# Layernorm's inverse deviation by a power on POOL, and gelu written out with Square and Tanh

## The chip, the cores and the metric

The kernel runs on one core of one Trainium2 chip. The metric is the device time of one execution in microseconds (us). Five engines work side by side, each through a list of instructions in a fixed order: TensorE (PE, with its weight loads shown apart as PEld), VectorE (DVE), ScalarE (ACT), GpSimd (POOL) and SyncE (SP, which here issues DMAs). They wait for each other through semaphores.

## The reference

Two transformer layers are run over x of shape (2, 1024, 256), with a context of shape (2, 77, 256). Every sublayer is preceded by a layernorm without weights:

```
def _layernorm(x, axis=-1, eps=1e-05):
    m = jnp.mean(x, axis=axis, keepdims=True)
    v = jnp.var(x, axis=axis, keepdims=True)
    return (x - m) / jnp.sqrt(v + eps)

x = x + L0_xattn(_layernorm(x), ctx)      # cross attention, 16 heads of 16, 77 keys, mask
x = x + L0_ffn(_layernorm(x))             # self attention with 4 heads of 16 chosen by a router
h = jnp.einsum('eth,efh->etf', _layernorm(x), ctx)
x = x + jnp.einsum('etf,efh->eth', jax.nn.gelu(h, approximate=True), ctx)
x = x + moe(_layernorm(x))                # top-1 of 8 experts, 256 -> 1024 -> 256, relu
```

The third sublayer is a feed-forward network whose weights are the context itself: 77 hidden units, with the approximate (tanh) gelu between two matmuls.

## The kernel before, in words

Everything is float32 apart from one mask matmul. The rows are held in SBUF as `xs`, 16 tiles of 128 rows by 256 features, 8 tiles for each of the two batches (`b`). The program runs these stages:

- start: weights are turned on TensorE, and layernorm `a` of batch 0 is written out in two halves of 4 tiles (L399 and L417);
- for each batch: `cross_attention(b)` (with layernorm `a` of batch 1 at its head), then layernorm `b`, then `route_heads(b)`, which averages the normalised rows, makes the router's softmax, picks four heads on VectorE (`nm`, `lg`, `top`, `idx`, `fi`, ..., `seli`) and has SP fetch their weights;
- for each batch: `self_attention(b)`, `context_ffn(b)` (layernorm `c` and the gelu) and `expert_logits(b)` (layernorm `d`, which also writes the normalised and the plain rows to the DRAM tensor `ztok`);
- the ranking of tokens by expert, and the expert blocks, which gather rows from `ztok`.

One layernorm (`layernorm`, `ln_stats`, `ln_rows`, `ln_turn`) works so: for each of 8 tiles VectorE makes statistics (`bn_stats`, `bn_aggr`, into `mv`); ScalarE takes the square root of the 8 variances at once (`sd`, L261); VectorE takes the reciprocal (`rs`, L262) and normalises tile by tile (`y`, L266); TensorE turns each pair of tiles (`lps`, L276), and ScalarE and VectorE in turn copy the result to `yT`. In layernorm `d`, SP writes each `y` to `ztok`, and ScalarE's queue issues the DMA of the plain rows (L297).

The gelu stage handles a batch in two chunks of 512 rows. Each makes `gps` (77 x 512, two matmuls in float32, L782), applies the gelu on ScalarE (`g`, L787), makes four products `gpo` (L790) and adds each to `xs` on VectorE (L794). `gps` and `gpo` share a PSUM pool of two buffers (`accp`), as do most small products.

ScalarE needs the table of a function in place before it can evaluate it. The compiler puts a load (ACT_TABLE_LOAD in the profile) ahead of an instruction whose function is not in the loaded set, and the profile gives it that instruction's line. In the program before there are loads ahead of Sqrt (L261), of Exp (L503, L559, L836), of the gelu (L787) and of the first copy (L370).

POOL has few instructions in the stages of the change: `add_bias` (L303), one addition over 8 tiles (128 x 2048) that must wait until the batch's rows have been read by the layernorm ahead of it, and copies of inverse sums in the self attention.

The order of instructions on each engine is made when the program is built: a planner orders them by estimated times, except in the two stretches under `manual_schedule` (the start and the self attention), where TensorE, VectorE and ScalarE keep the written order. A change of one instruction can thus move others. Once built, the order is fixed.

Of the kernel before, what the change touches and what calls it, by code (L numbers as in the profile page):

```python
# [9 lines left out]
F32 = mybir.dt.float32  # L10
# [3 lines left out]
AF = mybir.ActivationFunctionType  # L14
ALU = mybir.AluOpType
# [5 lines left out]
P = 128  # L21
EPS = 1e-5
NEG = -1e10


def bf16_parts(v):

    parts = []
    for _ in range(3):
        m, e = math.frexp(v)  # L30
        part = math.ldexp(math.trunc(m * 256), e - 8)
        parts.append(part)
        v -= part
    assert v == 0
    return parts
# [3 lines left out]
def kernel(  # L39
# [30 lines left out]
    nc = tc.nc  # L70
# [4 lines left out]
    NT = S // P  # L75
# [20 lines left out]
    const = ctx.enter_context(tc.tile_pool(name="const", bufs=1))  # L96
    keep = ctx.enter_context(tc.tile_pool(name="keep", bufs=1))
    small = ctx.enter_context(tc.tile_pool(name="small", bufs=2))
# [71 lines left out]

    ident = const.tile([P, P], F32, name="ident")
    make_identity(nc, ident)
    eps_t = const.tile([P, 1], F32, name="eps_t")
    nc.vector.memset(eps_t, EPS)


    ztok = dram.tile([B * S, 2 * D], F32, name="ztok")

    hmask = const.tile([P, HG], F32, name="hmask")
    nc.gpsimd.memset(hmask, float(HD) ** -0.5)
# [31 lines left out]
    neg3 = const.tile([P, 1], F32, name="neg3")  # L214
    parts = bf16_parts(NEG)
    nc.gpsimd.memset(neg3, 0.0)
# [36 lines left out]
    ynp = work.enter_context(tc.tile_pool(name="ynp", bufs=4))  # L253


    def ln_stats(b, tag, mv, sd, rs, t0, t1):
        for t in range(t0, t1):
            st = small.tile([P, 6], F32, name=f"st_{tag}{b}_{t}", tag="st", bufs=4)
            nc.vector.bn_stats(st, xs[:, b * NT + t, :])
            nc.vector.bn_aggr(mv[:, t, :], st)  # L260
        nc.scalar.activation(sd[:, t0:t1], mv[:, t0:t1, 1], AF.Sqrt, bias=eps_t)  # L261
        nc.vector.reciprocal(rs[:, t0:t1], sd[:, t0:t1])  # L262

    def ln_rows(b, tag, mv, rs, t):
        y = ynp.tile([P, D], F32, name=f"y_{tag}{b}_{t}", tag="y")
        nc.vector.tensor_scalar(  # L266
            y, xs[:, b * NT + t, :], mv[:, t, 0:1], rs[:, t : t + 1],
            ALU.subtract, ALU.mult,
        )
        return y  # L270

    def ln_turn(b, tag, yT, t0, ys, copy):
        ps = trp.tile([P, C, 2, P], F32, name=f"lps_{tag}{b}_{t0}", tag="tr")
        for i, y in enumerate(ys):
            for c in range(C):
                nc.tensor.transpose(ps[:, c, i, :], y[:, c * P : (c + 1) * P], ident)  # L276
        copy(yT[:, :, t0 * P : (t0 + 2) * P], ps.rearrange("p c t k -> p c (t k)"))

    def ln_tiles(b, tag):
        mv = small.tile([P, NT, 2], F32, name=f"mv_{tag}{b}", tag="mv")  # L280
        sd = small.tile([P, NT], F32, name=f"sd_{tag}{b}", tag="sd")
        rs = small.tile([P, NT], F32, name=f"rs_{tag}{b}", tag="rs")
        yT = ytp.tile([P, C, S], F32, name=f"yT_{tag}{b}", tag="yT")
        return mv, sd, rs, yT

    def layernorm(b, tag, y_out=None):

        mv, sd, rs, yT = ln_tiles(b, tag)
        ln_stats(b, tag, mv, sd, rs, 0, NT)
        for t0 in range(0, NT, 2):  # L290
            ys = []
            for t in (t0, t0 + 1):
                ys.append(ln_rows(b, tag, mv, rs, t))
                if y_out is not None:
                    r0 = (b * NT + t) * P
                    nc.sync.dma_start(y_out[r0 : r0 + P, :D], ys[-1])
                    nc.scalar.dma_start(y_out[r0 : r0 + P, D:], xs[:, b * NT + t, :])  # L297
            ln_turn(b, tag, yT, t0, ys, evac)
        return yT
# [42 lines left out]
    def queries(b, yT, n):  # L342

        for m in range(C):
            ps = accp.tile([P, 512], F32, name=f"qps_{b}_{m}_{n}", tag="acc")
            for c in range(C):
                nc.tensor.matmul(
                    ps,
                    lhsT=wT["q"][:, c, m * P : (m + 1) * P],
                    rhs=yT[:, c, n : n + 512],  # L350
                    start=(c == 0),
                    stop=(c == C - 1),
                )
            nc.scalar.activation(
                qT[:, m, n : n + 512], ps, AF.Identity, bias=bq_c[:, m : m + 1]
            )
# [4 lines left out]
    def turn_weight(nm, copy):  # L361

        t = wT[nm] = const.tile([P, C, D], F32, name=f"w{nm}T")
        ps = trp.tile([P, C, C, P], F32, name=f"wps_{nm}", tag="tr")
        for ci in range(C):
            for co in range(C):
                nc.tensor.transpose(
                    ps[:, ci, co, :], raw[nm][:, co, ci * P : (ci + 1) * P], ident
                )
        copy(t.rearrange("p c d -> p (c d)"), ps.rearrange("p a b k -> p (a b k)"))  # L370
# [8 lines left out]
    def context_k(m, eng):  # L379
        ps = accp.tile([P, B, KC], F32, name=f"kps_{m}", tag="acc")  # L380
        for c in range(C):
            nc.tensor.matmul(
                ps.rearrange("p b k -> p (b k)"),
                lhsT=wT["k"][:, c, m * P : (m + 1) * P],
                rhs=ctxT[:, c].rearrange("p b k -> p (b k)"),
                start=(c == 0),
                stop=(c == C - 1),
            )
        kT = small.tile([P, B, KC], F32, name=f"kT_{m}", tag="kT")
        nc.vector.scalar_tensor_tensor(kT, ps, bk_c[:, m : m + 1], keep01, ALU.add, ALU.mult)  # L390
        for j in range(HG):
            eng.tensor_scalar(kblk[:, :, m, j, :], kT, hmask[:, j : j + 1], None, ALU.mult)

    mv, sd, rs, yT_a = ln_tiles(0, "a")
    with tc.manual_schedule(
        engines={mybir.EngineType.PE, mybir.EngineType.DVE, mybir.EngineType.Activation}
    ):
        turn_weight("q", nc.scalar.copy)
        ln_stats(0, "a", mv, sd, rs, 0, 4)  # L399
        ys = [ln_rows(0, "a", mv, rs, t) for t in range(4)]  # L400
        for b in range(B):
            ps = trp.tile([P, C, KC], F32, name=f"cps_{b}", tag="tr")
            for c in range(C):
                nc.tensor.transpose(ps[:, c, :], ctxs[:, b, c * P : (c + 1) * P], ident[:KC, :KC])
            nc.scalar.copy(ctxT[:, :, b, :], ps)
        turn_weight("k", nc.scalar.copy)
        ln_turn(0, "a", yT_a, 0, ys[:2], nc.scalar.copy)
        ln_turn(0, "a", yT_a, 2, ys[2:], nc.scalar.copy)
        nc.vector.tensor_scalar(keep01, mask_i, 0.0, None, ALU.not_equal)
        context_k(0, nc.vector)  # L410
        context_k(1, nc.gpsimd)
        for j in range(HG):
            nc.vector.tensor_scalar(
                mneg[:, :, j, :], mask_i, 0.0, neg3, ALU.is_equal, ALU.mult
            )
        queries(0, yT_a, 0)
        ln_stats(0, "a", mv, sd, rs, 4, 8)  # L417
        ys = [ln_rows(0, "a", mv, rs, t) for t in range(4, 8)]
        ln_turn(0, "a", yT_a, 4, ys[:2], nc.scalar.copy)
        ln_turn(0, "a", yT_a, 6, ys[2:], nc.vector.tensor_copy)  # L420
        queries(0, yT_a, 512)
# [3 lines left out]
    for b in range(B):  # L425
        ps = accp.tile([KC, D], F32, name=f"vcps_{b}", tag="acc")
        for c in range(C):
            nc.tensor.matmul(
                ps, lhsT=ctxT[:, c, b, :], rhs=wT["v"][:, c, :], start=(c == 0), stop=(c == C - 1)
# [347 lines left out]
    def context_ffn(b):  # L777
        yT = layernorm(b, "c")
        for n in range(0, S, 512):
            ps = accp.tile([KC, 512], F32, name=f"gps_{b}_{n}", tag="acc")  # L780
            for c in range(C):
                nc.tensor.matmul(  # L782
                    ps, lhsT=ctxT[:, c, b, :], rhs=yT[:, c, n : n + 512],
                    start=(c == 0), stop=(c == C - 1),
                )
            g = ap_.tile([KC, 512], F32, name=f"g_{b}_{n}", tag="g")
            nc.scalar.activation(g, ps, AF.Gelu_apprx_tanh)  # L787
            for k in range(4):
                po = accp.tile([P, D], F32, name=f"gpo_{b}_{n}_{k}", tag="acc")
                nc.tensor.matmul(  # L790
                    po, lhsT=g[:, k * P : (k + 1) * P], rhs=ctxs[:, b, :], start=True, stop=True
                )
                xt = xs[:, b * NT + n // P + k, :]
                nc.vector.tensor_tensor(xt, po, xt, ALU.add)  # L794

    ps = trp.tile([P, E * FC], F32, name="b1ps", tag="tr")
    nc.tensor.transpose(ps, b1r, ident[: E * FC, : E * FC])
# [44 lines left out]
    for b in range(B):  # L842
        cross_attention(b)
        yT = layernorm(b, "b")
# [13 lines left out]
    ps = accp.tile([P, T + 1, E], F32, name="rank_ps", tag="acc")  # L858
# [219 lines left out]
```

## Time and profile before

| | |
|---|---|
| median of 3 runs | 691.75 us (690.45 to 695.22) |
| the profiled execution, its own time | 688.27 us |
| its span | 686.5 us |
| mean granted TensorE clock | 0.932 |
| PE busy | 602.5 us (88%), 3645 matmuls |
| PEld busy | 434.2 us (63%) |
| DVE busy | 384.6 us (56%), 874 instructions |
| ACT busy | 216.8 us (32%), 416 instructions |
| POOL busy | 80.6 us (12%), 119 instructions |

The profile is of one execution. A busy TensorE is not one at its peak: its clock can be granted in full (1.00) or in part, and a matmul that waits for a buffer inside a group is merged with its neighbours in the timeline. Groups of instructions are given as line, engine, operation, output <- input, count, then busy time in us, the mean of one in ns, and the engine's idle time just before them with what ended most of it. In the timeline the first two columns are the start and the length in us. Idle time of an engine that is not the limit costs nothing.

By stage, from the trace: the start runs to 30 us, cross attention and routing of both batches to 185, the self attention of batch 0 to 307, gelu and layernorm `d` of batch 0 to 340, the self attention of batch 1 to 471, gelu and layernorm `d` of batch 1 to 503, ranking to 518, the experts to the end.

### The profile page before, as it was taken

The page shows a single profiled execution, that of the slowest core. Times are in us where ns is not written, and L with a number is a line of the kernel's source. Part 1 is how long each engine was busy: PE and PEld are TensorE (multiplying, and loading weights), DVE is VectorE, ACT ScalarE, POOL GpSimd, SP SyncE. Part 2 cuts the span into 40 slices and gives each one's busy share as a digit, 9 for nine tenths or more (in the row PEclk, how much of TensorE's full clock was granted, in tenths as well). Part 3 has the DMA queues.
Part 4 walks back from the last instruction along what each step waited for, and adds up shares of the span by engine and source line. Part 5 has one row for each costly group of instructions (what it writes and reads, how often), then busy time and mean ns, then how long its engine had stood idle before and what let it go on. Part 6 is the DMA issues. An engine that isn't in the chain of part 4 may idle for free. (4 is left out here: it accounts for less than half of the span.)

```text
span 686.5 us, 9833 instructions
## 1 busy us (share of the span) xinstructions
PE 602.5 (88%) x3645; PEld 434.2 (63%) x3645; DVE 384.6 (56%) x874; ACT 216.8 (32%) x416; POOL 80.6 (12%) x119
## 2 busy tenths in 40 slices
PE   5799769995989999987999999998744999999985
PEld 3478645883455555553655555564544998899984
DVE  4599796986546666646455566665560322332421
ACT  3343224332036645523105555542200211111110
POOL 4300050002000000000000000000012122322311
PEclk9999969998999999998799999999655999999998
DMA  8000002000100000001100000000339599999980
GB/s 239 1 1 1 1 0 48 8 1 0 34 21 1 1 1 2 0 1 61 63 0 1 1 1 1 1 0 1 123 111 341 181 330 351 348 373 349 333 308 13
DMA packets 50822, 62.71 MB, mean 91 GB/s; under 512 B 12664, under 2 KB 43859, under 8 KB 50773
## 3 DMA queue, kind: packets, MB, share of 16 engines
q1 hardware_dynamic: 45200, 51.93, 22.8%
q0 software_dynamic: 2560, 7.34, 2.9%
q10 hardware_dynamic: 3013, 2.78, 1.2%
q8 instruction: 30, 0.49, 0.3%
q14 instruction: 19, 0.16, 0.1%
HBM read 55.75 MB, written 6.82 MB: 91 GB/s over the span
## 5 line engine op out<-in xcount | busy, mean ns | idle before, releaser
L680 DVE TENSOR_REDUCE bnm<-bsc 128x1 f32<-128x1024 f32 x64 | 75.4, 1219 | 49.5 <-PE bsc L666 49.5
L682 ACT ACTIVATE be<-bsc,bnm 128x1024 f32<-128x1024 f32 x64 | 70.9, 1112 | 50.3 <-DVE bnm L680 49.2
L692 PEld LDWEIGHTS bpt<-ident,be 128*128 128x128 f32 x512 | 54.9, 140 | 39.0 <-issue 18.6
L998 PE MATMUL ph<-ybT,w1s 128*128 128x128 f32 x640 | 76.6, 279 | 0.0
L998 PEld LDWEIGHTS ph<-ybT,w1s 128*128 128x128 f32 x640 | 74.9, 195 | 2.6 <-DVE ybT L993 2.4
L666 PE MATMUL bsc<-kT,qT 64*128 64x512 f32 x256 | 72.3, 640 | 3.5 <-ACT be L682 3.5
L1015 PE MATMUL epo<-w2s,ehT 128*128 128x256 f32 x320 | 75.2, 379 | 0.0
L1006 DVE TENSOR_SCALAR ehT<-ph,b1s 128x128 f32<-128x128 f32 x80 | 22.5, 344 | 93.7 <-ACT ehT L1004 93.7
L692 PE MATMUL bpt<-ident,be 128*128 128x128 f32 x512 | 70.7, 280 | 3.0 <-DVE beT L693 2.0
L1004 ACT ACTIVATE ehT<-ph,b1s 128x128 f32<-128x128 f32 x80 | 22.9, 369 | 149.5 <-issue 107.8
L693 ACT COPY beT<-bpt 128x512 f32<-128x512 f32 x64 | 37.5, 586 | 89.8 <-PE bpt L692 89.8
L702 PE MATMUL bov<-beT,v 128*64 128x256 f32 x512 | 62.3, 385 | 0.0
L1015 PEld LDWEIGHTS epo<-w2s,ehT 128*128 128x128 f32 x320 | 57.9, 190 | 6.3
L693 DVE COPY beT<-bpt 128x512 f32<-128x512 f32 x64 | 43.5, 684 | 17.2 <-PE bpt L692 17.2
L702 PEld LDWEIGHTS bov<-beT,v 128*64 128x64 f32 x512 | 34.3, 136 | 19.2 <-issue 5.7
L666 PEld LDWEIGHTS bsc<-kT,qT 64*128 64x128 f32 x256 | 26.4, 192 | 29.8 <-issue 19.5
L714 POOL COPY brb<-brc 128x256 f32<-128x256 f32 x16 | 6.4, 402 | 288.9 <-DVE brc L712 202.3
L521 PE MATMUL av<-vblk,eT 128*128 128x51 f32 x320 | 38.9, 269 | 0.1
L521 PEld LDWEIGHTS av<-vblk,eT 128*128 128x128 f32 x320 | 38.1, 192 | 0.9 <-PE po_a L338 0.9
L503 ACT ACTIVATE e<-e 128x616 f32<-128x616 f32 x32 | 23.0, 718 | 37.8 <-DVE e L499 37.8
L1024 POOL DMA_INDIRECT out_dram<-ob,etok x20 | 20.3, 1013 | 85.1 <-DMA out_dram<-ob,etok 64.4
L497 DVE TENSOR_REDUCE mx<-sc 128x8 f32<-128x616 f32 x32 | 25.2, 787 | 4.9 <-PE sc L488 4.6
(227 smaller groups left out, 790.9 us busy)
## 6 DMA issues: line engine op xcount, KB each, us to landing
w1s<-in_L_ffn_w_dram SPq DMA_DIRECT2D x20, 1024.0 KB, 10.4
w2s<-in_L_ffn_w_dram SPq DMA_DIRECT2D x20, 1024.0 KB, 9.8
b2s<-in_L_ffn_b_dram SPq DMA_DIRECT2D x20, 128.0 KB, 9.8
xs<-in_x_dram SPq DMA_DIRECT2D x4, 512.0 KB, 5.8
ztok<-xs ACTq DMA_DIRECT2D x16, 128.0 KB, 1.8
ztok<-y_d SPq DMA_DIRECT2D x16, 128.0 KB, 1.9
ws_q<-in_L_ffn_Wq_dram SPq DMA_DIRECT2D x8, 64.0 KB, 2.0
ws_k<-in_L_ffn_Wk_dram SPq DMA_DIRECT2D x8, 64.0 KB, 2.0
```

The source lines that it names most:

```text
L497: nc.vector.tensor_reduce(mx, scv, AX.X, ALU.max)
L503: nc.scalar.activation(em, em, AF.Exp)
L521: nc.tensor.matmul(av[:, h0 : h0 + HW, :].rearrange("p h d -> p (h d)"), lhsT=eT[:, c, :], rhs=vblk[:, b, c].rearrange("p h d -> p (h d)") ...
L666: nc.tensor.matmul(sc[h][:, n : n + 512], lhsT=qk["q"][m][r, t * P : (t + 1) * P], rhs=qk["k"][m][r, n : n + 512], start=True, stop=True,)
L680: nc.vector.tensor_reduce(nm, sc[h], AX.X, ALU.max, negate=True)
L682: nc.scalar.activation(es[i][:, h], sc[h], AF.Exp, bias=nm, accum_out=sms[g][:, q, s : s + 1])
L692: nc.tensor.transpose(pt[:, k - k0, :], es[i][:, h, k * P : (k + 1) * P], ident)
L693: copy(eTs[gm][:, h, k0 : k0 + 4, q * P : (q + 1) * P], pt)
L702: nc.tensor.matmul(ovs[gm][h * FD : (h + 1) * FD, :], lhsT=v[:, k, 2 * m + h, :], rhs=eTs[gm][:, h, k, :], start=(k == 0), stop=(k == NT - 1),
L998: nc.tensor.matmul(ph[:, f, :], lhsT=ws[n][0][:, c, f * P : (f + 1) * P], rhs=ybT[:, c, :], start=(c == 0), stop=(c == C - 1),)
L1004: nc.scalar.activation(hT[:, f, :], ph[:, f, :], AF.Relu, bias=b1s[:, f : f + 1])
L1015: nc.tensor.matmul(po, lhsT=hT[:, f, :], rhs=w2s[:, f, :], start=(f == 0), stop=(f == FC - 1))
```

## The change

Two edits. In `ln_stats`, VectorE adds the epsilon to the variances and POOL raises the sums to the power -0.5, with a constant tile `minus_half`; the square root on ScalarE and the reciprocal on VectorE go. In `context_ffn`, the gelu function of ScalarE is replaced by its formula, h/2 * (1 + tanh(sqrt(2/pi) * (h + 0.044715 h^3))): Square on ScalarE, a two-input step on VectorE, Tanh on ScalarE, another two-input step on VectorE; the half is applied in the addition to `xs`.

```
+    minus_half = const.tile([P, NT], F32, name="minus_half")
+    nc.gpsimd.memset(minus_half, -0.5)
...
-    def ln_stats(b, tag, mv, sd, rs, t0, t1):
+    def ln_stats(b, tag, mv, rs, t0, t1):
         for t in range(t0, t1):
             st = small.tile([P, 6], F32, name=f"st_{tag}{b}_{t}", tag="st", bufs=4)
             nc.vector.bn_stats(st, xs[:, b * NT + t, :])
             nc.vector.bn_aggr(mv[:, t, :], st)
-        nc.scalar.activation(sd[:, t0:t1], mv[:, t0:t1, 1], AF.Sqrt, bias=eps_t)
-        nc.vector.reciprocal(rs[:, t0:t1], sd[:, t0:t1])
+        nc.vector.tensor_scalar(rs[:, t0:t1], mv[:, t0:t1, 1], EPS, None, ALU.add)
+        nc.gpsimd.tensor_tensor(rs[:, t0:t1], rs[:, t0:t1], minus_half[:, t0:t1], ALU.pow)
...
             g = ap_.tile([KC, 512], F32, name=f"g_{b}_{n}", tag="g")
-            nc.scalar.activation(g, ps, AF.Gelu_apprx_tanh)
+            nc.scalar.activation(g, ps, AF.Square)
+            nc.vector.scalar_tensor_tensor(g, g, 1 / GELU_C, ps, ALU.add, ALU.mult)
+            nc.scalar.activation(g, g, AF.Tanh, scale=math.sqrt(2 / math.pi) * GELU_C)
+            nc.vector.scalar_tensor_tensor(g, g, 1.0, ps, ALU.add, ALU.mult)
...
-                nc.vector.tensor_tensor(xt, po, xt, ALU.add)
+                nc.vector.scalar_tensor_tensor(xt, po, 0.5, xt, ALU.mult, ALU.add)
```

`GELU_C` is 0.044715. The tiles `eps_t` and `sd` go. In the built program, ScalarE's list has one table load (L370), POOL's list has nine powers and one memset more, and the power of batch 1's layernorm `a` stands on POOL's list between the two bias additions of that stage. SP's list is the same.

More of the change, by code (lines that the diff above doesn't have):

```diff
@@ L23 @@
 NEG = -1e10
+GELU_C = 0.044715
 def bf16_parts(v):
@@ L172 @@
     make_identity(nc, ident)
-    eps_t = const.tile([P, 1], F32, name="eps_t")
-    nc.vector.memset(eps_t, EPS)
     ztok = dram.tile([B * S, 2 * D], F32, name="ztok")
+    minus_half = const.tile([P, NT], F32, name="minus_half")
+    nc.gpsimd.memset(minus_half, -0.5)
     hmask = const.tile([P, HG], F32, name="hmask")
@@ L280, in ln_tiles @@
         mv = small.tile([P, NT, 2], F32, name=f"mv_{tag}{b}", tag="mv")
-        sd = small.tile([P, NT], F32, name=f"sd_{tag}{b}", tag="sd")
         rs = small.tile([P, NT], F32, name=f"rs_{tag}{b}", tag="rs")
         yT = ytp.tile([P, C, S], F32, name=f"yT_{tag}{b}", tag="yT")
-        return mv, sd, rs, yT
+        return mv, rs, yT
     def layernorm(b, tag, y_out=None):
-        mv, sd, rs, yT = ln_tiles(b, tag)
-        ln_stats(b, tag, mv, sd, rs, 0, NT)
+        mv, rs, yT = ln_tiles(b, tag)
+        ln_stats(b, tag, mv, rs, 0, NT)
         for t0 in range(0, NT, 2):
@@ L392, in context_k @@
             eng.tensor_scalar(kblk[:, :, m, j, :], kT, hmask[:, j : j + 1], None, ALU.mult)
-    mv, sd, rs, yT_a = ln_tiles(0, "a")
+    mv, rs, yT_a = ln_tiles(0, "a")
     with tc.manual_schedule(
@@ L398 @@
         turn_weight("q", nc.scalar.copy)
-        ln_stats(0, "a", mv, sd, rs, 0, 4)
+        ln_stats(0, "a", mv, rs, 0, 4)
         ys = [ln_rows(0, "a", mv, rs, t) for t in range(4)]
@@ L416 @@
         queries(0, yT_a, 0)
-        ln_stats(0, "a", mv, sd, rs, 4, 8)
+        ln_stats(0, "a", mv, rs, 4, 8)
         ys = [ln_rows(0, "a", mv, rs, t) for t in range(4, 8)]
```

## The prediction

> **What bounds the kernel now.** I read the page first. TensorE is busy for 602.5 of the 686.5 us of the span, so no other engine's total decides; what decides is where TensorE stands still, or runs slowly, for the layernorms and the gelu. The page's chain that ended last covers only the last few microseconds, so it does not help here. Next I read ScalarE's groups by line, for what the change takes away:
>
> ```profile
> L261 ACT ACT_TABLE_LOAD x7 | 9.0, 1283 | 6.7 <-DMA ztok<-xs 6.6
> L559 ACT ACT_TABLE_LOAD x2 | 2.6, 1283 | 0.0
> L787 ACT ACT_TABLE_LOAD x2 | 2.6, 1283 | 0.0
> L836 ACT ACT_TABLE_LOAD x2 | 2.6, 1283 | 0.0
> ```
>
> With one load each at L503 and L370 there are 15 loads, 1283 ns each. In the built order of the changed program only L370's is left: 14 go, 14 x 1.283 = 18.0 us of ScalarE. Are they on the path? The timeline of the first gelu stage (start, length, engine, line; idle before it and what ended it, in brackets):
>
> ```profile
> 302.39 1.28 ACT L261 ACT_TABLE_LOAD   x1
> 307.12 0.30 ACT L261 ACTIVATE sd_c<-mv_c,eps_t 128x8 f32<-128x8 f32 x1 [3.45 <-DVE mv_c L260]
> 307.45 0.20 DVE L262 RECIPROCAL rs_c<-sd_c 128x8 f32<-128x8 f32 x1 [0.37 <-ACT sd_c L261]
> 311.31 1.28 ACT L787 ACT_TABLE_LOAD   x1
> 314.13 0.59 ACT L787 ACTIVATE g<-gps 77x512 f32<-77x512 f32 x1 [1.54 <-PE gps L782]
> 314.77 2.35 PE L790 MATMUL gpo<-ctxs,g 77*128 77x256 f32 x8 [0.68 <-ACT g L787]
> 317.20 1.94 PE L782 MATMUL gps<-yT_c,ctxT 128*77 128x512 f32 x4
> 319.18 0.59 ACT L787 ACTIVATE g<-gps 77x512 f32<-77x512 f32 x1 [4.46 <-DMA ztok<-xs]
> ```
>
> Both loads end before what ScalarE waits for: 3.45 us of idleness follow one, 1.54 us the other. They are hidden. The gelu itself is not: TensorE waits 0.68 us for each of its four runs, and nothing else is in its queue.
>
> Only the layernorm after the gelu has its load on the path, because ScalarE comes to it late, behind four DMA issues:
>
> ```profile
> 323.08 1.28 ACT L261 ACT_TABLE_LOAD   x1 [3.30 <-DMA ztok<-xs]
> 323.67 0.30 DVE L260 BATCH_NORM_AGGREGATE mv_d<-st_d 128x2 f32<-128x6 f32 x2
> 324.38 0.30 ACT L261 ACTIVATE sd_d<-mv_d,eps_t 128x8 f32<-128x8 f32 x1
> 324.95 0.41 DVE L266 TENSOR_SCALAR y_d<-xs,mv_d,rs_d 128x256 f32<-128x256 f32 x1
> ```
>
> **Part 1: the loads.** Statistics end at 323.97 and the square root could start at once, but starts at 324.38: 0.41 us, twice, so 0.8 us of the 18.0 are on the path (counted in part 2's layernorm d). The others are covered: the first L261 load (7.40) by the arrival of raw_k, for which TensorE waits until 9.53; L503's by VectorE's first softmax rows, 3.65 us later; those of layernorm b (78.60 and 156.00) by 2.50 and 2.31 us of idleness behind them; L559's and L836's by 3.5 to 5.1 us of idleness. Without that cover each would cost 1.28 us.
>
> The Trainium skill, "ScalarE: Activation LUTs", section "What ACT_TABLE_LOAD costs", puts a switch at about 1283 ns plus a drain of about 1380 ns; in this trace the root at 8.69 follows the load of 7.40 without a gap, so only the first part shows. By that page 14 switches would be an estimated 37 us of ScalarE, by the row 18.0; the page does not ask what hides them.
>
> **Part 2: the inverse deviation.** Before: root on ScalarE (0.30), reciprocal on VectorE (0.20), about 0.6 us from the last statistics to the first normalised row. After: add on VectorE (0.17, as the small TENSOR_SCALAR rows), power on POOL, and two hand-offs of about 0.05. No row shows a power. Below, a two-input POOL row: 128x2048 takes 4.51 us and 128x64 (L982) 0.40 us, which is 2.07 ns an element above 0.27, so 0.29 us for 8 elements if a power cost as much as an add. Above, the longest two-input row itself, 4.5 us. L982 is the nearest row; with twenty times its price an element the power takes 0.27 + 0.33 = 0.6 us, and I take that. Then 0.17 + 0.10 + 0.6 = 0.88 us.
>
> Place by place: layernorm a of batch 0, first half: covered by raw_k, 0. Second half: 17.85 to 18.55 was 0.70 us, now 0.9: +0.2. b of batch 0: the reciprocal stood behind six bn_stats of batch 1 (84.14, though the root was done at 82.68); in the built order two of those still come ahead, so up to 1 us is gained there, but statistics that moved behind it eat most of it before the routing sums: 0. b of batch 1: 159.55 to 160.16, +0.3. c: +0.3 twice. d: the load's 0.41 goes, 0.98 becomes 0.9: -0.1 for both.
>
> Layernorm a of batch 1 is different, for VectorE's order changes. Today:
>
> ```profile
> 97.64 4.51 POOL L303 TENSOR_TENSOR xs<-xs,bo_b 128x2048 f32<-128x2048 f32 x1 [5.05 <-DVE top L565]
> 97.97 4.22 DVE L569 CAST fi<-idx 128x4 f32<-128x4 uint32 x1
> 102.93 0.68 DVE L109 COPY yT_a<-lps_a 128x512 f32<-128x512 f32 x1
> ```
>
> A cast of 4 elements took 4.22 us and ended with POOL's bias addition; in batch 1 the same cast, with POOL idle, took 0.17. So VectorE's cast stands until POOL is done. In the built order all statistics of batch 1's a come later, the add and the power follow the routing maximum (94.3 instead of 91.5), and the rows are normalised between the routing steps: the first row starts near 95.2 instead of 92.66, the last ends near 100.4 instead of 97.57. The bias addition waits for that last row, runs until 104.9, and holds the routing's last cast (seli), which now stands ahead of the copy of yT_a. That copy ends near 105.7 instead of 103.6: +2.1 us for TensorE's queries. If that cast is not held, 0. On POOL's queue the power stands behind the other bias addition, which ends at 92.6, before the power's input is there. SP's list is unchanged.
>
> **Part 3: the gelu.** One ACTIVATE becomes Square, a two-input VectorE step, Tanh, and another such step, each waiting for the last; the halving rides on the existing addition (0.42 either way). ACTIVATE 0.59. VectorE: 256 elements from PSUM and SBUF take 0.42 (L794), 616 take 0.80 (L499), 1.04 ns an element above 0.16, so 0.69 for 512; the three-operand row L390 lies 0.06 above that line; I take 0.72. Hand-offs 0.03 (307.42 to 307.45). Added: 0.59 + 2 x 0.72 + 3 x 0.03 = 2.12 us, four times, 8.5 us. Both engines are free then. The four ztok issues on ScalarE's queue stay behind the second ACTIVATE, and move with it. TensorE's order in this stage does not change, so nothing fills the gap.
>
> **Part 4: TensorE's clock.** Stretches of 2 us; the third number from the end is the granted clock, the first after the stretch's length TensorE's busy time:
>
> ```profile
> 306.00:308.00 2.00, 0.00 (x0) 0.00 (x0) 1.56 (x7) 0.30 (x1) 0.00 (x0) 1.00 0.00 0
> 308.00:310.00 2.00, 1.80 (x10) 1.20 (x11) 2.00 (x7) 0.59 (x1) 0.00 (x0) 0.93 0.00 0
> 310.00:312.00 2.00, 2.00 (x6) 0.83 (x5) 0.96 (x3) 1.28 (x2) 0.00 (x0) 0.50 0.00 0
> 312.00:314.00 2.00, 2.00 (x7) 1.05 (x5) 0.69 (x1) 0.59 (x1) 0.00 (x0) 0.72 0.00 0
> ```
>
> A pause of 2.21 us (305.95 to 308.16) is followed by half clock from 309.7 to 313.1. Today's pauses of 0.68 us bring none between 313 and 323. They become 0.68 + 2.12 = 2.8 us. I expect one such stretch of 3.4 us more in each batch; at half clock up to half of it is lost, and TensorE also waits within it, so 1.5 us each: 3.0. Bounds: 0 and two stretches in each batch, 6.8.
>
> The Trainium skill, "TensorE: Matmul & The Clock Gate", section "HAM oscillation — how this bites in real kernels", forbids only TensorE pauses over about 3.4 us; by it the 2.8 us pauses cost nothing and the sum would be 3.0 lower. The row above, half clock after 2.21 us, speaks against it.
>
> **Sum.** 0.2 + 0.3 + 0.6 - 0.1 = 1.0 for the layernorms, 2.1 for the cast, 8.5 for the gelu, 3.0 for the clock: +14.6 us. The profiled execution took 688.27 us (span 686.5, 1.8 around it), so 702.9 for its like. It lies 3.5 below the median of the three runs, 691.75; I predict the median: 706.
>
> **Rivals.**
> *Light (699).* The power costs 0.29 (seven places on the path, -2.1), the cast is not held (-2.1), the clock holds (-3.0): +7.4. For it: from 314 to 320 TensorE is busy for 4.47 of 6 us, and the clock holds at 1.00. Against: the 4.22 us row and the row of half clock.
> *Slow power (740).* 4.5 us: 3.9 x 7 more, and the two covered places add some 3.4 and 3.2: +34 over the sum. For it: no row gives a power's price. Against: every POOL row of up to 154 elements is under 0.8 us, DMAs apart. Each 1 us more of power is 7 us.
> *Not slower (689): the loads were on the path after all.* If all 14 end waits, 18.0 - 0.8 = 17.2 come off: 706.4 - 17.2 = 689.2. It decides from twelve of fourteen loads. Against: the idle times after them, above.
> That the change keeps its loads is excluded by the built order: a single one is left.
>
> **How the numbers follow.** Forecast 0.60, light 0.17, slow power 0.20, loads 0.03. The range 698 to 722 holds the forecast with its bounds, the light case, and a power up to about 2.3 us; beyond lie some 0.13 above and 0.05 below. One per cent (6.9 us) is about what a measurement of this kernel tells from no change. Only the loads' case, or a lucky light one, is faster by over that: 0.03; within it lie the light case's lower half and the rest: 0.10; slower: 0.87.
>
> **What would show it.** Right: ScalarE has one table load; Square, VectorE, Tanh, VectorE stand in a row of about 2.7 us with TensorE waiting 2.8 us ahead of the gpo matmuls, four times; the power's row near 0.6 us; the cast of seli near 4 us beside POOL's bias addition; half clock between the two gelu runs. Wrong: a power over 2 us; TensorE's wait ahead of the gelu's second matmul under 2 us; layernorm stages shorter than now.

## The result, and the profile after

The changed kernel takes 718.57 us (median of 5 runs, 716.4 to 731.58) against 691.75: a ratio of 1.040 [1.037, 1.0431]. The forecast was 706 with a range of 698 to 722: the direction and the range held, the size did not. Run again beside the kernel before it gave 1.0406 [1.0352, 1.046]. That repeat's profile is read here (span 718.8, own time 720.6), because in the first profiled execution the expert stage alone was about 12 us longer, which no other run shows.

The groups by line (busy us, mean ns of one; then the engine's idle time just before, and what ended it). Of the kernel before:

```profile
L790 PE MATMUL gpo<-ctxs,g 77*128 77x256 f32 x32 | 9.0, 405 | 3.1 <-ACT g L787 2.7
L276 PE MATMUL lps_d<-ident,y_d 128*128 128x128 f32 x32 | 7.7, 424 | 6.7 <-DVE y_d L266 6.7
L276 PE MATMUL lps_c<-ident,y_c 128*128 128x128 f32 x32 | 7.0, 356 | 4.5 <-DVE y_c L266 4.4
L276 PE MATMUL lps_b<-ident,y_b 128*128 128x128 f32 x32 | 6.2, 344 | 6.8 <-DVE y_b L266 6.7
```

Of the changed kernel:

```profile
L370 ACT ACT_TABLE_LOAD x1 | 1.3, 1283 | 2.5 <-issue 2.5
L263 POOL TENSOR_TENSOR rs_c<-rs_c,minus_half 128x8 f32<-128x8 f32 x2 | 3.3, 1642 | 15.4 <-DVE rs_c L262 15.4
L794 PE MATMUL gpo<-ctxs,g 77*128 77x256 f32 x32 | 12.1, 531 | 11.3 <-DVE g L791 11.1
L277 PE MATMUL lps_d<-ident,y_d 128*128 128x128 f32 x32 | 8.2, 425 | 8.6 <-DVE y_d L267 8.6
L277 PE MATMUL lps_b<-ident,y_b 128*128 128x128 f32 x32 | 7.2, 375 | 8.2 <-DVE y_b L267 8.1
L277 PE MATMUL lps_c<-ident,y_c 128*128 128x128 f32 x32 | 6.9, 384 | 7.2 <-DVE y_c L267 7.2
```

One table load is left of 15, as the built order said. A power of 128x8 takes 1.64 us. TensorE waits 11.1 us for the gelu, 2.7 before.

The timeline of the first gelu stage, after:

```profile
314.73 0.17 DVE L262 TENSOR_SCALAR rs_c<-mv_c 128x8 f32<-128x8 f32 x1
314.98 1.65 POOL L263 TENSOR_TENSOR rs_c<-rs_c,minus_half 128x8 f32<-128x8 f32 x1 [7.70 <-DVE rs_c L262]
316.66 2.04 DVE L267 TENSOR_SCALAR y_c<-xs,mv_c,rs_c 128x256 f32<-128x256 f32 x6 [1.77 <-POOL rs_c L263]
...
322.51 0.59 ACT L788 ACTIVATE g<-gps 77x512 f32<-77x512 f32 x1 [1.85 <-PE gps L782]
323.13 0.68 DVE L789 SCALAR_TENSOR_TENSOR g<-g,gps 77x512 f32<-77x512 f32 x1 [0.79 <-ACT g L788]
323.85 0.63 ACT L790 ACTIVATE g<-g 77x512 f32<-77x512 f32 x1 [0.75 <-DVE g L789]
324.51 0.68 DVE L791 SCALAR_TENSOR_TENSOR g<-g,gps 77x512 f32<-77x512 f32 x1 [0.70 <-ACT g L790]
325.25 2.64 PE L794 MATMUL gpo<-ctxs,g 77*128 77x256 f32 x8 [2.78 <-DVE g L791]
327.77 3.30 PE L782 MATMUL gps<-yT_c,ctxT 128*77 128x512 f32 x4
```

Two things are to be seen. VectorE stands for 1.77 us between its own addition and its first row, for POOL's power; root and reciprocal took 0.6 us in all. And the four steps of the gelu stand in a row from 322.51 to 325.19 with TensorE waiting beside them, 2.78 us.

Layernorm d of batch 0, after; the same stretch took 0.98 us from the statistics to the first row before, and takes 1.96 now (339.37 to 341.33):

```profile
339.40 0.17 DVE L262 TENSOR_SCALAR rs_d<-mv_d 128x8 f32<-128x8 f32 x1
339.65 1.64 POOL L263 TENSOR_TENSOR rs_d<-rs_d,minus_half 128x8 f32<-128x8 f32 x1 [23.03 <-DVE rs_d L262]
341.33 1.38 DVE L267 TENSOR_SCALAR y_d<-xs,mv_d,rs_d 128x256 f32<-128x256 f32 x4 [1.75 <-POOL rs_d L263]
341.89 1.94 PE L277 MATMUL lps_d<-ident,y_d 128*128 128x128 f32 x8 [4.31 <-DVE y_d L267]
```

The cast beside POOL's bias addition, in batch 1's layernorm a, after:

```profile
102.47 4.51 POOL L303 TENSOR_TENSOR xs<-xs,bo_b 128x2048 f32<-128x2048 f32 x1 [4.15 <-DVE at L580]
102.71 4.29 DVE L584 CAST seli<-sel 128x4 int32<-128x4 f32 x1
106.91 0.68 DVE L110 COPY yT_a<-lps_a 128x512 f32<-128x512 f32 x1
```

TensorE's clock in windows of the gelu stage and layernorm d, after (length, TensorE's busy time, ..., the granted clock third from the end):

```profile
326.00:328.00 2.00, 1.91 (x7) 0.85 (x6) 1.67 (x5) 0.00 (x0) 0.00 (x0) 0.79 0.27 89
328.00:330.00 2.00, 2.00 (x3) 0.58 (x3) 1.69 (x8) 0.00 (x0) 0.00 (x0) 0.50 0.51 173
332.00:334.00 2.00, 0.14 (x1) 0.14 (x2) 1.11 (x2) 0.63 (x1) 0.00 (x0) 1.00 0.00 0
346.00:352.00 6.00, 6.00 (x18) 3.69 (x16) 1.47 (x3) 0.21 (x1) 0.00 (x0) 0.50 0.20 67
358.00:360.00 2.00, 1.95 (x12) 1.36 (x11) 1.63 (x6) 0.00 (x0) 0.00 (x0) 1.00 0.00 0
```

A stretch of half clock (327 to 330.5) now lies between the two gelu runs, where there was none. A second, in layernorm d, lasts from 334 to about 358; before it lasted from 323.5 to 333.5.

How far the changed kernel lags behind the one before, at the start of some steps (from the two timelines):

| step | lag, us |
|---|---|
| first scores of batch 0 (L479 before) | 1.7 |
| layernorm b of batch 1, first transpose | 5.4 |
| layernorm c of batch 0 | 9.0 |
| layernorm d of batch 0 | 16.4 |
| first queries of batch 1's self attention | 20.7 |
| layernorm c of batch 1 | 22.2 |
| layernorm d of batch 1 | 29.8 |
| ranking | 31.3 |
| end of the span | 32.3 |

The matmuls are the same 3645, so the 32.3 us split by the page's first lines: TensorE's busy time grew from 602.5 to 616.5 (+14.0: the same matmuls, with the granted clock at 0.908 instead of 0.932) and its idle time by the other 18.3. (The profiled execution of before lies 3.5 us under its median, so by medians the difference is 27 to 28 us.) The idle time is found again in the waits ahead of three groups: the gelu's gpo 8.4 (2.7 to 11.1), the transposes of layernorms b, c and d 6.0 (6.8, 4.5, 6.7 to 8.2, 7.2, 8.6) and those of layernorm a 3.2 (2.5 to 5.7): 17.6 together.

### The profile page after: what moved, and what is told of

Same layout as the page of the kernel before. It is cut to its first block, busy times and chain, and to the rows that moved or that the text cites. A ratio compares the mean times of both kernels' runs of the same rounds, so it can differ in the third digit from the quotient of the medians.

```text
span 729.8 us, 9831 instructions
## 1 busy us (share of the span) xinstructions
PE 620.1 (85%) x3645; PEld 442.3 (61%) x3645; DVE 390.3 (53%) x881; ACT 198.9 (27%) x397; POOL 94.6 (13%) x129
## 3 DMA queue, kind: packets, MB, share of 16 engines
q10 hardware_dynamic: 3013, 2.78, 1.1%
## 5 line engine op out<-in xcount | busy, mean ns | idle before, releaser
L1002 PEld LDWEIGHTS ph<-ybT,w1s 128*128 128x128 f32 x640 | 76.8, 199 | 2.1 <-DVE ybT L997 1.2
L666 PE MATMUL bsc<-kT,qT 64*128 64x512 f32 x256 | 74.0, 639 | 3.5 <-ACT be L682 3.5
L693 DVE COPY beT<-bpt 128x512 f32<-128x512 f32 x64 | 43.7, 686 | 18.0 <-PE bpt L692 17.8
```

What stands on the lines that cost most here:

```text
L666: nc.tensor.matmul(sc[h][:, n : n + 512], lhsT=qk["q"][m][r, t * P : (t + 1) * P], rhs=qk["k"][m][r, n : n + 512], start=True, stop=True,)
L693: copy(eTs[gm][:, h, k0 : k0 + 4, q * P : (q + 1) * P], pt)
L1002: nc.tensor.matmul(ph[:, f, :], lhsT=ws[n][0][:, c, f * P : (f + 1) * P], rhs=ybT[:, c, :], start=(c == 0), stop=(c == C - 1),)
```

## The experiments

They ran on three chips, in groups of four; each ratio is to runs of the kernel before on the same chip, whose median was 692.69 us for the first group, 686.71 for the second and 690.22 for the third. Groups are compared by ratio.

### First group: the parts, one at a time

The changed kernel again, unedited:

> The changed kernel again, for a profile without the longer expert stage of the first one. Theory (a sum of five terms: gelu chain 8.5 us, half clock, power 1.65 us at seven places, moved VectorE steps, and almost nothing back for the loads): about 27 us over the kernel before, with the growth spread over all stages up to the ranking and none behind it (end of the ranking's first matmul about 28 to 31 us later than before, the experts as long as before). Rival (part of the loss lies in the expert stage, as the first profile shows 12 us there): the experts are longer here too.

719.71 us, ratio 1.0406 [1.0352, 1.046].

The gelu alone: the kernel before with only this edit; roots and loads stay.

```
-            nc.scalar.activation(g, ps, AF.Gelu_apprx_tanh)
+            nc.scalar.activation(g, ps, AF.Square)
+            nc.vector.scalar_tensor_tensor(g, g, 1 / GELU_C, ps, ALU.add, ALU.mult)
+            nc.scalar.activation(g, g, AF.Tanh, scale=math.sqrt(2 / math.pi) * GELU_C)
+            nc.vector.scalar_tensor_tensor(g, g, 1.0, ps, ALU.add, ALU.mult)
```

> The kernel before with only the gelu written out; root, reciprocal and all 15 table loads stay (one now stands between Square and Tanh), and TensorE's list is word for word that of before. Theory: 4 x 2.1 = 8.4 us of chain, 2 x 0.55 because the load of 1.28 is longer than the VectorE step of 0.72 beside it, and about 1.7 us of half clock in each batch: +13 us, between 10 and 15. Rival (clock not touched by pauses of 2.8 us): +9.5 us with granted clock 1.00 between the two gelu runs. Rival (second chunk's chain hides behind the first's products): under +5 us.

702.88 us, ratio 1.0188 [1.0133, 1.0244]: 13 us by the ratio (10 by the medians). The timeline of its first gelu run:

```profile
313.55 0.59 ACT L788 ACTIVATE g<-gps 77x512 f32<-77x512 f32 x1 [2.86 <-PE gps L783]
314.15 1.28 ACT L790 ACT_TABLE_LOAD   x1
315.45 0.63 ACT L790 ACTIVATE g<-g 77x512 f32<-77x512 f32 x1
316.85 3.81 PE L794 MATMUL gpo<-ctxs,g 77*128 77x256 f32 x8 [3.34 <-DVE g L791]
```

Here, and only here, a table load stands in the chain: 1.28 us beside VectorE's 0.68, so that TensorE waits 3.34 us instead of 2.78 once in each batch. These 1.1 us are this hybrid's own; without them the gelu costs about 12 us by the ratio.

The power alone: the changed kernel with the gelu function put back (five loads are left).

```
-            nc.scalar.activation(g, ps, AF.Square)
...
+            nc.scalar.activation(g, ps, AF.Gelu_apprx_tanh)
```

> The changed kernel with the gelu function put back: power on POOL, five table loads left. Theory: power 1.65 us, 1.4 us more than root and reciprocal at b and c of both batches, 0.6 at the second half of a, 1.0 at each d, 2.9 at batch 1's a with its held cast, and VectorE's kT step ahead of the last y_d, 3 to 4 us: +14 us, between 11 and 17. Rival (the power is nearly hidden and the gelu is the whole loss): under +4 us.

701.93 us, ratio 1.0156 [1.0101, 1.0212]: 10.8 us by the ratio (9.2 by the medians), where the prediction had 1.0 + 2.1 for this part. Not all of it is waiting: TensorE's busy time grew too, from 602.5 to 609.0 us. TensorE's groups of transposes, power alone:

```profile
L277 PE MATMUL lps_d<-ident,y_d 128*128 128x128 f32 x32 | 7.7, 407 | 8.6 <-DVE y_d L267 8.6
L277 PE MATMUL lps_b<-ident,y_b 128*128 128x128 f32 x32 | 7.7, 416 | 8.3 <-DVE y_b L267 8.3
L277 PE MATMUL lps_c<-ident,y_c 128*128 128x128 f32 x32 | 6.8, 377 | 7.1 <-DVE y_c L267 7.1
```

The waits are those of the whole change, so they belong to the power. The two ratios add up to 3.4 per cent, the change has 4.1: with intervals of half a per cent each, that is no evidence for more than a sum.

No loads: the kernel before with Identity in place of the root and Tanh in place of the gelu. It leaves out the root and the gelu's formula, so its output is another; and without the loads the planner also moves some VectorE steps, so this is not the loads alone.

```
-        nc.scalar.activation(sd[:, t0:t1], mv[:, t0:t1, 1], AF.Sqrt, bias=eps_t)
+        nc.scalar.activation(sd[:, t0:t1], mv[:, t0:t1, 1], AF.Identity, bias=eps_t)
...
-            nc.scalar.activation(g, ps, AF.Gelu_apprx_tanh)
+            nc.scalar.activation(g, ps, AF.Tanh)
```

> The kernel before with Identity (same bias) in place of Sqrt and Tanh in place of the gelu: the same number of instructions, but one table load instead of 15. It leaves out the square root and the gelu's formula, so the output is another. The planner, without the loads, moves the routing's last casts behind the rows of batch 1's a and VectorE's kT ahead of the last y_d, as in the changed kernel. Theory (loads hidden; only the moves count): between -2 and +5 us. Rival (the loads were on the path): -10 to -17 us.

691.67 us, ratio 0.9971 [0.9936, 1.0006]. Fourteen loads are gone, 18.0 us of ScalarE, and the time falls by 1 us of medians, by at most 4.4 us by the interval. TensorE's idle time in the profiles falls by 2.2 us (84.0 to 81.8); in it the moved steps show, for the wait ahead of layernorm a's transposes grows from 2.5 to 3.9 us and those of b and d shrink by 1.1 and 0.8.

The Trainium skill, "ScalarE: Activation LUTs", section "What ACT_TABLE_LOAD costs", prices each switch at about 2.66 us with its drain, an estimated 37 us for 14; the measurement decides: what a switch costs the kernel is what of it lies on the path, here at most 0.32 us each by the interval, with the moved steps in it.

### Second group: the gap, the price of a power, and an attempt at a remedy

The changed kernel with four matmuls whose result nobody uses in each of the gelu's waits, to keep TensorE busy:

```
             nc.scalar.activation(g, ps, AF.Square)
+            warm = trp.tile([P, 512], F32, name=f"warm_{b}_{n}", tag="tr")
+            for w in range(4):
+                rhs = yT[:, 0, n : n + D] if n == 0 else xs[:, b * NT + n // P - 1, :]
+                nc.tensor.matmul(warm[:, :D], lhsT=ident, rhs=rhs, start=True, stop=True)
```

> The changed kernel with four idle 128x256 matmuls (about 0.49 us each at full clock, result unused) in each of the gelu's four waits, after gps and before gpo; VectorE's list is unchanged. Theory (pauses of 2.8 us bring the half clock of the gelu stage): the clock stays at 1.00 from the first gelu to the last product, the second gps takes 1.94 us and not 3.5, the last products 2.35 and not 3.1 to 4.6: 2.5 us less in each batch, 4 to 6 us less than the changed kernel in all, although work was added. Rival (half clock has other reasons, or falls outside anyway): no change or up to 3 us more.

716.55 us, ratio 1.0416 [1.0352, 1.048]: no gain that the intervals show. The idle part of each wait fell from 2.78 to 1.05 us, and the stretch of half clock from 327.5 to 330 stayed (the granted clock is 0.76, 0.50 and 0.89 in the three windows of 2 us from 326 to 332). What did change is the one in layernorm d, which ended at about 351 instead of 358; from the mean clocks, (1 - 0.914) x 716.9 x 2 = 123 us of the span ran at half clock instead of 132. So, against the theory, filling these waits did not keep the clock, and what the run gained elsewhere is too little to show: inconclusive on the size.

Each power followed by a second one with the exponent 1:

```
         nc.gpsimd.tensor_tensor(rs[:, t0:t1], rs[:, t0:t1], minus_half[:, t0:t1], ALU.pow)
+        nc.gpsimd.tensor_tensor(rs[:, t0:t1], rs[:, t0:t1], plus_one[:, t0:t1], ALU.pow)
```

> The changed kernel with a second power on POOL after each of the nine (exponent 1, the same shapes: 1.65 us for 128x8, about 1.04 for 128x4). Theory (the power is on the path at seven or eight of nine places): 7 x 1.65 + 1.04 = 12.6 us more than the changed kernel, between 10 and 16. Rival (POOL's power runs beside other work): under 4 us more.

738.04 us, ratio 1.0725 [1.0675, 1.0776]. The spans of the two profiled executions differ by 17.5 us. Groups with the doubled power:

```profile
L280 PE MATMUL lps_d<-ident,y_d 128*128 128x128 f32 x32 | 8.2, 425 | 12.0 <-DVE y_d L270 12.0
L280 PE MATMUL lps_b<-ident,y_b 128*128 128x128 f32 x32 | 7.9, 426 | 11.6 <-DVE y_b L270 11.6
L280 PE MATMUL lps_c<-ident,y_c 128*128 128x128 f32 x32 | 7.4, 405 | 10.6 <-DVE y_c L270 10.6
```

TensorE's waits at the six places of b, c and d go from 8.2 + 7.2 + 8.6 = 24.0 to 34.2: 1.70 us a place, the second power (1.64 us) and its hand-off entire. Layernorm a adds 3.0. That is 13.2 us of waiting; TensorE's busy time is 5.5 longer (622.0), with the mean clock at 0.894 for 0.908. So at the places of b, c and d nothing covers a further power, batch 0's layernorm b included (4.03 to 5.75 us). Of layernorm a's 3.0 us, 1.26 lie ahead of the very first transposes. There the changed kernel's single power cost nothing: its transposes follow the matmuls on raw_k without a wait, as the prediction had said.

Both chunks' gps matmuls made first, in one PSUM tile:

```
+        gps = big.tile([KC, 2, 512], F32, name=f"gps_{b}", tag="big")
         for n in range(0, S, 512):
...
+        for n in range(0, S, 512):
+            ps = gps[:, n // 512, :]
             g = ap_.tile([KC, 512], F32, name=f"g_{b}_{n}", tag="g")
```

> The changed kernel, but gps of both chunks are made first, in one PSUM tile of another pool, so that the second chunk's four steps can run beside the first chunk's products; in the built order kT of the next batch is also no longer ahead of the last y_d. Theory (the chain costs because TensorE has nothing in between): the second wait of 2.8 us goes and the second gps (1.9 to 3.5) fills the first wait, 4.7 to 6.3 us less in each batch, and 2 to 4 us less for the moved kT: -11 to -16 us against the changed kernel. Rival (ScalarE's four ztok issues or VectorE's additions hold the second chain anyway): -4 us or less.

712.36 us, ratio 1.0364 [1.0314, 1.0414]: less than was expected of it. The timeline:

```profile
321.34 2.95 PE L782 MATMUL gps<-yT_c,ctxT 128*77 128x512 f32 x6
...
324.33 0.59 ACT L790 ACTIVATE g<-gps 77x512 f32<-77x512 f32 x1 [4.16 <-PE gps L782]
...
327.07 3.55 PE L796 MATMUL gpo<-ctxs,g 77*128 77x256 f32 x8 [2.78 <-DVE g L793]
```

The Square of the first chunk waits for the last matmul of the second (321.34 + 2.95 = 324.29): with one tile for both, reading a half waited for the whole. The work meant to fill the gap was put ahead of it, and TensorE still waits 2.78 us; only the second wait is gone. Of that, 2.4 us return in its groups as a longer wait ahead of layernorm d's transposes (11.0 us for 8.6).

The same with layernorm's statistics (L260 to L263) made in two halves of 4 tiles:

```
-        ln_stats(b, tag, mv, rs, 0, NT)
+        ln_stats(b, tag, mv, rs, 0, NT // 2)
+        ln_stats(b, tag, mv, rs, NT // 2, NT)
```

> As both_gps_first, and the layernorms b, c and d and batch 1's a make the inverse deviation in two halves of four tiles, so that the first half's power (1.04 us) runs while the last tiles' statistics are still waited for; without table loads the halves cost ScalarE nothing. Theory (the power costs only because it stands between the last statistics and the first row): a further 1 to 1.4 us less at six or seven places, -7 to -10 us against both_gps_first, -18 to -26 against the changed kernel, that is about the kernel before or just under it. Rival (the second half's power is the new wait, or the planner's order takes it back): within 3 us of both_gps_first.

701.3 us, ratio 1.0184 [1.0133, 1.0236]: 11.1 us less than without the halves, on the same chip. In the groups the waits ahead of the transposes of b, c and d fell by 12.1 us, from 26.4 (8.3, 7.1 and 11.0) to 14.3 (5.4, 1.5 and 7.4), and ahead of layernorm a's by 2.4. Part of that only moved: ahead of the gps matmuls, where TensorE did not wait, it now waits 3.8 us.

```profile
L783 PE MATMUL gps<-yT_c,ctxT 128*77 128x512 f32 x16 | 8.0, 601 | 3.8 <-DVE mv_c L261 2.0 <-DVE yT_c L110 1.8
```

The balance of the three is 10.7 us, close to the 11.1 of the times.

### Third group: the remedies apart

Two PSUM tiles in place of the one:

```
-        gps = big.tile([KC, 2, 512], F32, name=f"gps_{b}", tag="big")
+        gps = [
+            big.tile([KC, 2, 512], F32, name=f"gps_{b}_{n}", tag="big")[:, 0, :]
+            for n in range(0, S, 512)
+        ]
```

> The changed kernel with both chunks' gps matmuls made first, now each in a PSUM tile of its own (two of the pool named big). With one tile for both, the Square of the first chunk waited for the matmuls of the second, and TensorE still stood still for 2.78 us ahead of each batch's first gpo. Theory (TensorE's waits are the price of the gelu chain): the wait ahead of the first gpo falls from 2.78 to about 0.9 us, since the second chunk's gps (1.9 us at full clock) lies within it, the one ahead of the second stays near 0.2; four waits come to about 2.2 us instead of 11.1, and the kernel is some 4 us faster than with one tile: ratio 1.028 to 1.032. Rival (half clock takes back what the waits give, or the two buffers of gpo do): ratio 1.035 to 1.038, the waits gone all the same.

706.56 us, ratio 1.0225 [1.0194, 1.0257], better than either theory had it. The timeline:

```profile
323.34 0.59 ACT L793 ACTIVATE g<-gps 77x512 f32<-77x512 f32 x1 [1.84 <-PE gps L785]
...
326.08 2.35 PE L799 MATMUL gpo<-ctxs,g 77*128 77x256 f32 x8 [0.85 <-DVE g L796]
...
328.66 2.35 PE L799 MATMUL gpo<-ctxs,g 77*128 77x256 f32 x8 [0.23 <-DVE xs L803]
```

The waits are 0.85 and 0.23 us (0.85 and 0.17 in batch 1), and in batch 0 both gpo runs take 2.35 us, as at full clock (in batch 1 the second takes 3.81, at half clock). In its groups TensorE waits 2.4 us for gpo instead of 11.3, and 11.0 ahead of layernorm d instead of 8.6; its busy time is 612.1 us instead of 616.5. Against the changed kernel the ratio falls by 1.8 points, about what the written-out gelu had cost alone (1.9). That does not make the formula free. The power with the gelu function and no such help took a ratio of 1.0156, and the function gains from the two tiles as well: TensorE waits 0.5 us for it instead of 3.1 in the kernel of roots in halves below. What the formula costs beside the function when both have two tiles, no run shows.

The last row of batch 0's layernorm d on POOL:

```
+        eng = nc.gpsimd if (b, tag, t) == (0, "d", 7) else nc.vector
-        nc.vector.tensor_scalar(
+        eng.tensor_scalar(
```

> The changed kernel with the last row of batch 0's layernorm d (y_d of tile 7) normalised on POOL instead of VectorE; nothing else. In the changed kernel VectorE's kT step stands ahead of that row and waits 4.0 us for TensorE's bps_k, so that the row, the copy of its transposes and TensorE's last lps_d come late. Theory (that wait sets the end of the stage): from the first lps_d to the first bps_q of batch 0 it takes 13 to 14.5 us instead of 17.1, and the kernel is 3 to 4 us faster than the changed kernel, a ratio to the kernel before of 1.035 to 1.037. Rival (half clock and the write-back of the rows' buffers set it, and the kT step only fills a wait): 16 to 17 us for the stretch, ratio 1.040.

719.21 us, ratio 1.0419 [1.0392, 1.0447]. The timeline:

```profile
347.84 1.24 POOL L268 TENSOR_SCALAR y_d<-xs,mv_d,rs_d 128x256 f32<-128x256 f32 x1 [5.46 <-DVE y_d L268]
...
351.79 1.92 PE L278 MATMUL lps_d<-ident,y_d 128*128 128x128 f32 x8
352.03 0.75 DVE L628 TENSOR_SCALAR kT<-bps_k,bc_k 128x512 f32<-128x512 f32 x1 [4.22 <-PE bps_k L621]
```

The row no longer waits for kT, and its transposes run with those before them; the stretch from the first lps_d (342.98) to the first bps_q (360.51) still takes 17.5 us. The theory falls, the rival stands: from 346.5 on TensorE is busy without a pause at half clock, and what VectorE waits for beside it is covered.

The kernel before, with statistics in halves and both gps first in two tiles (root, reciprocal, gelu function):

> The kernel before (root on ScalarE, reciprocal, gelu function) with two edits: layernorm's statistics, root and reciprocal in two halves of 4 tiles, and both chunks' gps made first in two PSUM tiles. The rows of a layernorm can start 4 statistics (about 2.1 us) earlier. Theory (a layernorm's latency ahead of TensorE's first transpose is on the path, whatever makes the inverse deviation): 1 to 2 us less at each of seven places and about 2 us less in the gelu stage: 10 us faster than the kernel before, ratio 0.980 to 0.990. Rival (twice as many roots bring table loads onto the path): ratio 0.995 to 1.005.

683.34 us, ratio 0.99 [0.9859, 0.9941]: faster than both kernels, at the near end of what was expected. Its groups (from an execution of 678.03 us, 5.3 under the median):

```profile
L261 ACT ACT_TABLE_LOAD x10 | 12.8, 1283 | 6.4 <-DMA ztok<-xs 6.3
L276 PE MATMUL lps_c<-ident,y_c 128*128 128x128 f32 x32 | 4.7, 277 | 0.0
L786 PE MATMUL gps<-yT_c,ctxT 128*77 128x512 f32 x16 | 7.6, 600 | 2.0 <-DVE mv_c L260 2.0
L796 PE MATMUL gpo<-ctxs,g 77*128 77x256 f32 x32 | 8.8, 396 | 0.5 <-DVE xs L800 0.4
```

It has 21 table loads in all, six more than the kernel before, and TensorE waits next to nothing for the gelu. The waits ahead of all transposes fall from 20.5 to 13.3 us, those for the gelu's products from 3.1 to 0.5; layernorm c's have not all gone, 2.0 us now stand ahead of the gps matmuls (0.2 before).

The same two edits with the power on POOL and the gelu function:

> The same two edits (statistics in halves, both chunks' gps first in two tiles) with the power on POOL, and the gelu function on ScalarE. Theory: the power of a second half lies beside the rows of the first half and costs nothing; that of a first half (4 elements, 1.04 us, with the addition and hand-offs about 1.3 against 0.6) stays on the path: 7 x 0.7 = 4.9 us over the kernel with roots in halves, and 1.7 us for the order of batch 0's layernorm d: 6 to 7 us, 0.9 to 1.0 per cent over it, so a ratio to the kernel before of about 0.995. Rival (in halves the power is hidden wholly): within 0.3 per cent of the kernel with roots in halves. Second rival (its price stays as in whole layernorms, 1.05 us at each of seven places and more): 1.5 per cent over it.

687.44 us, ratio 0.9954 [0.993, 0.9979]. Its groups:

```profile
L263 POOL TENSOR_TENSOR rs_c<-rs_c,minus_half 128x4 f32<-128x4 f32 x4 | 4.0, 1009 | 19.1 <-DVE rs_c L262 19.1
L277 PE MATMUL lps_c<-ident,y_c 128*128 128x128 f32 x32 | 4.9, 277 | 1.5 <-DVE y_c L267 1.5
```

The waits ahead of all transposes are 17.8 us, 4.5 above those with the root (4.9 were expected), and 1.8 more stand ahead of the gps matmuls (3.8 for 2.0). The time is 0.54 points above, 4.1 us of medians; the two intervals overlap a little, so the size is uncertain. One half's power is covered and the other's is not, but not always as the theory had it. In layernorm d the rows wait for the first half's. In layernorms b and c the first half's statistics and power are done while the stage ahead still runs, and it is the second half's for which VectorE, and TensorE behind it, wait:

```profile
160.79 1.01 POOL L263 TENSOR_TENSOR rs_b<-rs_b,minus_half 128x4 f32<-128x4 f32 x1 [8.89 <-DVE rs_b L262]
161.83 1.38 DVE L267 TENSOR_SCALAR y_b<-xs,mv_b,rs_b 128x256 f32<-128x256 f32 x4 [1.12 <-POOL rs_b L263]
```

Whether the 1.7 us expected for the order of layernorm d are among them, these numbers cannot tell.

## Why the prediction was right, and where it was not

*Part 1, the loads.* Right. 14 of 15 went; they were covered. The case without loads bounds their worth, together with the steps that moved, at 4.4 us, and 21 loads did not keep another kernel from being the fastest here.

*Part 2, the power.* The step that failed is the price: 0.6 us was taken for 128x8 and 1.64 measured. The prediction added 0.27 us to twenty times an addition's 2.07 ns an element; from 128x4 (1.01 us) and 128x8 (1.65) it is about 0.16 us an element above 0.4, some 77 times an addition's. Its rule "each 1 us more of power is 7 us" gives 7.3 for the 1.04 missed; power alone cost 10.8 by its ratio against 3.1, so 7.7 more. That these agree so well is partly luck, for the 10.8 hold some clock too; TensorE's waits ahead of the transposes grew by 9.2 us where 3.1 were put, so by 6.1 more. Batch 0's layernorm b, put at 0, lost 0.12 (a wait of 4.03 for 3.91): four fewer of batch 1's statistics now stand ahead there, the gain that the prediction had set against the power. *Layernorm d* was to gain 0.1 and lost 1.0, for the same price.

*Layernorm a of batch 1.* Right in mechanism and size: the cast took 4.29 us for a predicted 4, and the lag grew from 2.1 (the routing sums of batch 0) to 4.0 (the first scores of batch 1), 1.9 for a predicted 2.1. The cast ends with POOL's addition (107.00 and 106.98). The size is partly luck: the power in this term took 1.04 us longer than the prediction had put, and by its own rule the lag should have grown by some 3.1.

The Trainium skill, "SBUF — State Buffer", section "SBUF: two separate sides", says that VectorE, for instructions in a 2-port mode or with two SBUF inputs, and GpSimd share one pair of ports, locked for a whole instruction, with the other fully blocked. The 4.29 us row agrees; which accesses of the cast take the shared pair no row here says.

*Part 3, the gelu.* Right to a tenth: predicted 2.12 us more in each wait, measured 2.10 (0.68 to 2.78); four of them 8.4 for 8.5. Nothing filled the gap, as said; the runs add that another order and a second tile fill most of it (0.85 and 0.23 us).

*Part 4, the clock.* Right for the stretch that it named, wrong in leaving out the others. The stretch between the gelu runs came, 3.5 us in batch 0 and again in batch 1, and the matmuls in it took about 3.2 us longer in both together (in batch 0 gps 3.30 for 1.94 and gpo 2.64 for 2.35, in batch 1 gps 3.45 for 1.94). But 3.0 us were put for the clock and TensorE's busy time grew by 14.0 between the two profiled executions, some 10 if the 3.5 us by which that execution of before lies under its median are taken off. What the sum left out are the stretches elsewhere: a new one at 20 to 23 us (after a pause of 2.29 us where there were 1.63), and 24 us of half clock in layernorm d of batch 0 for 10 before. From the mean clocks of the two profiled executions, 132 us ran at half clock instead of 93; by the medians of all fast runs it was 133 instead of 100, so that execution of before had less of it than most. By the same medians the gelu alone has 116 us, the power alone 113 and the kernel without loads 104: each edit brings about half, the loads' going next to none.

That a pause of TensorE brings the half clock, on which the prediction's step rests, is not shown. With two tiles and the waits down to 0.85 us, the stretch was gone from batch 0's gelu runs but came in batch 1's (from 498.7 us); with the waits filled down to 1.05 us it stayed in both.

The Trainium skill, "TensorE: Matmul & The Clock Gate", section "HAM oscillation — how this bites in real kernels", speaks of pauses over about 3.4 us. As a threshold for the pause just ahead, the trace does not agree with it: half clock stands behind pauses of 2.3 and 2.8 us, as it did behind the 2.21 us of before.

*The sum.* 11.6 us of waits became 18.3 and 3.0 of clock some 10: +28 instead of +14.6. The forecast's side was chosen rightly, on the gelu's chain. Its range held because it had room for a power of 2.3 us; the clock's share went past its own bound of 6.8, so that the range held is in part luck. Of the rivals, the light case fell with the power and the clock; the slow power had the right direction, and the power took about a third of the 4.5 us that it supposed; the loads' case fell.

What stays open: why the half clock in batch 0's layernorm d lasts 10, 13 or 24 us. It lasted 24 us in the changed kernel and with two tiles, 13 with the filled gap and with the power alone; TensorE's pause ahead of layernorm d's transposes was 4.3, 5.5, 4.3 and 4.3 us. No run separates the causes.

## What to carry to other kernels

A step that frees an engine is worth what it takes off the path, and a table load behind which its engine idles is worth little (here at most 4.4 us for fourteen); price instead the latency that the replacement puts between two matmuls, with a bound for an operation whose row you lack. A chain of small steps between matmuls costs its whole length unless TensorE has other work queued beside it, in a tile of its own. Where a layernorm's statistics hold up the first transpose, do them in halves: with the power on POOL that took 1.8 points off the ratio, about as much as the written-out gelu had put on.

## What the runs showed of the hardware that was not expected

- POOL's power depends steeply on the elements for so small a tile: 1.01 us for 128x4, 1.65 for 128x8, where an addition of 128x64 takes 0.40.
- A TensorE that the profile shows as busy is not enough for its clock to rise. With two tiles, from 338 to 351 us it was busy for 13.00 of 13 us and the granted clock stayed at 0.50 (many of its matmuls there have only 8 columns):

```profile
338.00:351.00 13.00, 13.00 (x48) 10.31 (x47) 3.99 (x10) 0.84 (x2) 0.00 (x0) 0.50 0.20 65
```

- Matmuls put into a pause to keep the clock up (1.9 us of each 2.8) did not keep it: the half-clock stretch that followed stayed where it was.
